# Attention followed by a binarised convolution: the order of the 5x5 products, and where the partial sums are joined

## The chip, the cores and the metric

The kernel runs on one core of one Trainium2 chip. The metric is the device time of one execution in microseconds (us), as the median of three runs. A profile is one further execution, recorded instruction by instruction. Its engines are called PE (TensorE, matmuls; PEld is its weight load), DVE (VectorE), ACT (ScalarE), POOL (GpSimd) and SP (SyncE, which here only issues DMAs).

## What is computed

The input x is 8 images of 64 channels and 64 x 64 pixels, fp32. Two layers follow one another:

```python
# layer 0: attention over the n = 4096 pixels of an image
q, k, v = wq @ xf + bq, wk @ xf + bk, wv @ xf + bv
q_mean, k_mean = q.mean(pixels), k.mean(pixels)
sim = softmax((q - q_mean).T @ (k - k_mean) / 8)
out = sim @ v + v @ softmax(q_mean @ (k - k_mean))   # second term: one vector per image
x = x + out
# layer 1: three binarised convolutions, summed, gated by channel
s = 0
for kk in (1, 3, 5):
    y = sign(x + move_kk)
    z = conv_kk(y, scale * sign(w_kk - mean(w_kk)), padding="SAME")
    s += z * inv_kk + shift_kk                          # batch norm
gate = sigmoid(grouped_linear(mean(s, pixels)))         # channels shuffled
out = s * gate + x
```

## The kernel before

Two images make a pair: their 2 x 64 channels fill the 128 partitions, so there are four pairs. A pair's 4096 pixels are cut into 8 blocks of 512 columns (8 image rows). The outer loop in `attend` runs over the 32 blocks g of all pairs, numbered from 0; the inner one over 32 slots j, one for each 128 keys.

In slot j PE computes `scores` (L472) into a bank pair `ps` of the pool `ps_s`, which has two such buffers, and then `weighted` (L491) for the slot before, which accumulates into `acc`, the only buffer of `ps_a`. ScalarE turns ps into the tile `e` by an exp (L483). VectorE adds each e into `es` (L506), for the softmax's denominators. Matmuls are 64 x 64, so four of them, one for each quarter of the array, run at a time; PE takes them from one queue in program order. In the text, a "stream" is the matmuls that use one half of the array's rows.

Everything else is hung into the slots by `plan`, an explicit table of which function is called after the matmuls of which slot. `put(i, f)` puts f into slot i. The order in which the functions issue their instructions is the order on each engine.

Slot 0 of block g holds `weighted_out` for block g - 1 (ScalarE copies acc to SBUF, L513), the DMAs for the denominators, and then `mix_rows`. This issues one run of matmuls that mixes the queries of block g + 1 (`pq`) with the convolution of block g - 3. Such a convolution is done for blocks g = 3 to 31, so 29 times. Row sums and differences of the signs halve the work: a pair of image rows is put together from four products, named A, B, S and D. The even row of a pair is A + S/2 + D/2 and the odd row -B + S/2 - D/2 (factors `frac`, L206). Each product has 256 columns, two rows' worth of four row pairs.

The PSUM tiles of a convolution are these. z_5 lies in a score buffer of `ps_s` and holds the 5x5's S, A and B. z_5d holds its D and lies in a bank of the pool `ps_m` (two banks). z_3 is the 3x3's A, B, S, D in the buffer of `ps_a`, that is, in the place of acc. z_1, the 1x1 convolution, is in the other bank of `ps_m`. The two banks of `ps_m` are used in turn: first the two query tiles, then the two convolution tiles.

`mix_rows` makes two sequences, `seqs[0]` and `seqs[1]`, for the two streams, and merges them by a running cost: 2.0 for a query, 0.5 for a product, 1.0 for the 1x1. Before the change the first holds 8 products of the 5x5's S, the twelve of the 3x3, the last 2 of S and the 1x1. The second holds 6 of A, the five of D, 4 of A, ten of B.

The sum `sb` of a block is built in this order. When z_5d is complete, `begin_rows` (L719) starts sb with it by two ScalarE operations, one for even and one for odd rows. When z_3 is complete, `hold_rows` (L744) copies it to an SBUF tile, `es_z`, which frees the acc buffer. After the last matmul, `add_rows` (L737) adds S (two operations, even and odd rows), A and B of the 5x5 on VectorE, which frees the score buffer. In slots 7, 8 and 9 `add_held` adds the 3x3's four products from es_z by six more such operations. In slot 10 `end_rows` (L753) adds the 1x1 and accumulates the sum over all pixels into a column of `gap`, for the gate.

The means of a pair come from eight partial sums of its x, made by ScalarE in slots 14 to 28 of an earlier block (L274). `mean_scores`, in slot 0 of blocks 4, 12 and 20, behind `mix_rows`, reduces the eight columns to `xm` on VectorE (L286) and multiplies by a matrix on PE (`pm`, L288). The query tiles are read out right after their matmuls, one by VectorE (`q`, L465) and one by ScalarE (L466). In slot 0 of blocks 1, 8, 16 and 24, behind `mix_rows`, two more small matmuls (`po`, L361 and L362) end a pair's second attention term; VectorE takes the reciprocal of a sum `su` from them and ScalarE checks it (L416).

```python
put(0, both)
if qb == 4 and pr + 1 < n_pairs:
    put(0, lambda: nx().mean_scores(8))
...
    put(7, p3.add_held, b3, "AB")
    put(8, p3.add_held, b3, "S")
    put(9, p3.add_held, b3, "D")
    put(10, p3.end_rows, b3)
```

Of the kernel before, what the change touches and what calls it, by code (L numbers as in the profile page):

```python
# [22 lines left out]
ALU = mybir.AluOpType  # L23
# [21 lines left out]
def conv_seq_kernel(ctx, tc, x, wq, wk, wv, vecs, w1, w3, w5, wtap, gw, out):  # L45
# [211 lines left out]
    class Pair:  # L257
# [3 lines left out]
        def __init__(self, name, xt):  # L261
            self.name, self.x = name, xt
            self.xs = sm.tile([P, 8], F32, tag="xs", name=f"xs_{name}")
            self.q, self.x2, self.s, self.y1, self.acc = {}, {}, {}, {}, {}
            self.es, self.r, self.joint, self.sc = {}, {}, None, None

# [15 lines left out]

        def mean_scores(self, parts=4):

            xm = self.tile(sm, "xm", 0, (P, 1))
            nc.vector.tensor_reduce(xm, self.xs[:, 0:parts], AX.X, ALU.add)  # L286
            self.pm = m_tile(f"pm_{self.name}")
            nc.tensor.matmul(self.pm[:, 0:1], mm, xm, start=True, stop=True)  # L288

# [419 lines left out]
        def sum_tile(self, qb):  # L709
            return bp.tile([P, QB], F32, tag="sb", bufs=9, name=f"sb_{self.name}_{qb}")  # L710

        def begin_rows(self, qb, z):

            self.s[qb] = self.sum_tile(qb)
            if qb == 0:
                self.gap = self.tile(sm, "gap", 0, (P, NQ + 1))
            sv = self.s[qb].rearrange("p (j t w) -> p j t w", t=2, w=HH)
            for t in range(2):
                nc.scalar.activation(  # L719
                    sv[:, :, t, :],  # L720
                    z.rearrange("p (j w) -> p j w", w=HH),
                    AF.Identity,
                    bias=shift,
                    scale=frac[5][:, t : t + 1],
                )

        def add_rows(self, qb, k, name, z):
            sv = self.s[qb].rearrange("p (j t w) -> p j t w", t=2, w=HH)
            f = {
                "A": {0: scale[:, k // 2 : k // 2 + 1]},  # L730
                "B": {1: frac[k][:, 2:3]},
                "S": {0: frac[k][:, 0:1], 1: frac[k][:, 0:1]},
                "D": {0: frac[k][:, 0:1], 1: frac[k][:, 1:2]},
            }[name]
            for t, by in f.items():
                out = sv[:, :, t, :]
                nc.vector.scalar_tensor_tensor(  # L737
                    out, z.rearrange("p (j w) -> p j w", w=HH), by, out, ALU.mult, ALU.add
                )

        def hold_rows(self, qb, two):

            self.z3 = self.tile(sm, "es", f"z3_{qb}", (P, 2, QB))
            nc.scalar.copy(self.z3, two)  # L744

        def add_held(self, qb, names):
            for n in names:
                i = "ABSD".index(n)
                self.add_rows(qb, 3, n, self.z3[:, i // 2, bass.ts(i % 2, QB // 2)])

        def end_rows(self, qb):
            s = self.s[qb]
            nc.vector.scalar_tensor_tensor(  # L753
                s, self.z1, scale[:, 0:1], s, ALU.mult, ALU.add, accum_out=self.gap[:, qb : qb + 1]
            )

        def rows(self, qb):

            return qb * ROWS, ROWS, self.y1[qb], qb

        def joint_rows(self, r0, r1, i):
            y = [t[:, r0 * HH : r1 * HH] for t in self.joint[0]]
            return N // HH - 2 * ROWS + r0, r1 - r0, y, NQ - 2 + i

        def conv_tap(self, rows, z, b, h, n, i, first, last):


            r0, nr, y, _ = rows
# [13 lines left out]

        def convs_out(self, rows, z, n):
            r0, nr, _, col = rows
            w = nr * HH
            qb, at = divmod(r0 * HH, QB)
            if n == 0:
                if qb not in self.s:
                    self.s[qb] = self.sum_tile(qb)
                if qb == 0:  # L790
                    self.gap = self.tile(sm, "gap", 0, (P, NQ + 1))
            s = self.s[qb]
            if self.joint is not None and qb >= NQ - 2:
                s, at = self.joint[1], at + (qb - NQ + 2) * QB
            s = s[:, at : at + w]
            if n == 0:
                nc.scalar.activation(s, z[0][0][:, 0:w], AF.Identity, bias=shift, scale=scale[:, 0:1])
                return
            for h in range(len(z[n])):
                gap = dict(accum_out=self.gap[:, col : col + 1]) if (n, h) == (2, 1) else {}  # L800
                nc.vector.scalar_tensor_tensor(
                    s, z[n][h][:, 0:w], scale[:, n : n + 1], s, ALU.mult, ALU.add, **gap
                )

        def gate_mean(self):
            self.ga = self.tile(sm, "ga", 0, (P, 1))
            some = NQ + (self.joint is not None)
            nc.vector.tensor_reduce(self.ga, self.gap[:, 0:some], AX.X, ALU.add)

# [64 lines left out]
    def mix_rows(q, c):  # L874
# [6 lines left out]
        if c is not None:  # L881
            p, (r0, _, y, qb) = c

            def products(k, name):
                return [((k, name), i, 0.5) for i in range(n_products(k, name))]

            S, A = products(5, "S"), products(5, "A")
            three = [t for name in "ABSD" for t in products(3, name)]
            seqs[0] += S[:8] + three + S[8:] + [((1,), 0, 1.0)]
            seqs[1] += A[:6] + products(5, "D") + A[6:] + products(5, "B")  # L890
        order = []
# [12 lines left out]
        for _, h, b, (n, i, _) in order:  # L904
            if n == ("q",):
                q[0].split_queries(q[1], b, h)
            else:
# [13 lines left out]
                if n == (1,):  # L921
                    p.conv_tap((r0, ROWS, y, qb), [[z[n]]], b, 0, 0, 0, True, True)
                else:
                    p.row_product(z[n], b, *n, i, r0)
            left[n] -= 1
            if left[n] == 0 and n == ("q",):
                q[0].split_queries_out(q[1])
            elif left[n] == 0 and n == (5, "D"):
                p.begin_rows(qb, z[n])
            elif left[n] == 0 and n == (3, "D"):  # L930
                p.hold_rows(qb, z3)
        if c is not None:
            for n in "SAB":
                p.add_rows(qb, 5, n, z[5, n])
            p.z1 = z[1,]

# [20 lines left out]
    def attend(pairs):  # L957
# [9 lines left out]
        def plan(g):  # L967
# [25 lines left out]
            if qb == 4 and pr + 1 < n_pairs:  # L993
                put(0, lambda: nx().mean_scores(8))
                put(0, lambda: nx().mean_scores_out())
                put(1, lambda: nx().value_weights())
# [5 lines left out]
            if g >= 3:  # L1002
                p3, b3 = block(g - 3)
                put(7, p3.add_held, b3, "AB")
                put(8, p3.add_held, b3, "S")
                put(9, p3.add_held, b3, "D")
                put(10, p3.end_rows, b3)
# [43 lines left out]
            if pr + 1 < n_pairs:  # L1051
# [5 lines left out]
                if qb == (3 if pr == 0 else 2):  # L1057
                    for c in range(8):
                        cols = slice(c * QB, (c + 1) * QB)
                        put(14 + 2 * c, lambda c=c, cols=cols: nx().mean_part(c, cols, True))  # L1060
                if qb >= 4:
                    for h in range(2):
# [5 lines left out]
            if g == n_blocks - 1:  # L1068
                put(1, pairs[-1].join)
                put(22, lambda: mix(None, rows(n_blocks - 3), one_bank, score_banks))  # L1070
                put(27, lambda: mix(None, (pairs[-1], pairs[-1].joint_rows(0, 6, 0)), one_bank, score_banks))
            return at
# [33 lines left out]
        for (r0, r1), cols in zip(parts, halves):  # L1106
# [6 lines left out]
            p.signs(b, r0, r1, nc.gpsimd.tensor_copy)  # L1113
        mix(None, (p, p.joint_rows(6, 11, 1)), one_bank, score_banks)
        mix(None, (p, p.joint_rows(11, 16, 2)), one_bank, score_banks)
        p.check(p.r[b], n_blocks - 1)
# [12 lines left out]
    with tc.manual_schedule():  # L1129
# [14 lines left out]
        warm(18)  # L1144
        first.mean_scores(5)
        first.mean_scores_out()
# [16 lines left out]
    with tc.If(n_good < P):  # L1163
        neg = fp.tile([P, QB], F32, tag="e5", name="neg")
        nc.vector.memset(neg, 0.0)
        with tc.For_i(0, n_pairs * P, P) as row:
            rows = bass.ds(row, P)
            p = Pair("g", load_x("g", rows))
            for c in range(4):
                p.mean_part(c, quarters[c])  # L1170
            p.mean_scores()
            p.mean_scores_out()
# [107 lines left out]
```

## Time and profile before

| what | us |
|---|---|
| median of three runs | 1950.62 |
| lowest and highest run | 1950.45, 1952.43 |
| the profiled execution's own time | 1954.38 |
| its span, first to last instruction | 1952.2 |
| PE busy | 1923.2 (99%) |
| DVE busy | 1617.6 (83%) |
| ACT busy | 1275.4 (65%) |
| L506, the additions to es, 960 | 1172.3 |
| L737, `add_rows`, 290 in all | 131.7 |
| L719, `begin_rows`, 58 | 29.6 |
| L744, `hold_rows`, 29 | 29.4 |
| L753, `end_rows`, 29, with its 29 accumulator reads | 24.4 |

A line of the timeline gives the start, the length, the engine, the source line, the operation, what is written and read, the shapes, and how many instructions are merged into the line; in brackets stands how long the engine was idle before it and what it waited for. A fp32 matmul of the kernel is recorded as two instructions, so one slot's scores are eight.

### The profile page before, as it was taken

To read this page: it belongs to the slowest core of one execution; us is meant where nothing else is said; L and a number is where in the kernel's file an instruction comes from. 1 tells how busy PE (TensorE), PEld (TensorE's weight loads), DVE (VectorE), ACT (ScalarE), POOL (GpSimd) and SP (SyncE) were. 2 spreads that over 40 slices of the span, in tenths; PEclk is the share of its full clock that TensorE was granted. 3 is DMA by queue.
4 is the path that set the end of the run, shared out by engine and by line. 5 is a ranking of instruction groups with operands and counts; after the bars stand their busy time and mean duration, and the time that the engine had idled before them with its cause. 6 is when DMAs were issued, how large, how long until landed. Compare 5 with 4: busy or idle time off the path is not lost.

```text
span 1952.2 us, 48415 instructions
## 1 busy us (share of the span) xinstructions
PE 1923.2 (99%) x20848; PEld 800.4 (41%) x20848; DVE 1617.6 (83%) x2066; ACT 1275.4 (65%) x1552; POOL 5.9 (0%) x26
## 2 busy tenths in 40 slices
PE   9999999999999999999999999999999999999997
PEld 4333434443344443444434444344443444444444
DVE  6878878889887888888888888888888888878876
ACT  5667766666666766666666676666666666666663
POOL 0000000000000000000000000000000000000000
PEclk9999999999999999999999999999999999999999
DMA  3021111110102111111011211011111011111111
GB/s 100 31 63 33 29 36 35 38 33 19 40 31 83 56 48 29 36 35 35 28 28 40 80 56 56 16 40 36 35 35 32 23 51 49 55 39 33 28 34 46
DMA packets 58998, 80.58 MB, mean 41 GB/s; under 512 B 15628, under 2 KB 40600, under 8 KB 58648
## 3 DMA queue, kind: packets, MB, share of 16 engines
q1 hardware_dynamic: 58024, 76.22, 12.8%
q8 instruction: 165, 2.70, 0.6%
q10 hardware_dynamic: 720, 1.18, 0.2%
q14 instruction: 57, 0.47, 0.1%
q0 software_dynamic: 32, 0.01, 0.0%
HBM read 39.27 MB, written 24.77 MB: 33 GB/s over the span
## 4 chain that ended last, share of the span: by engine, by line
PE 94%; DVE 3%; ACT 1%; issue 1%; DMA 0%; DVEq 0%; SPq 0%
PE ps L472 44%; PE acc L491 44%; PE z L701 3%; DVE sb L737 2%; PE pv L311 1%; PE pq L458 1%; PE z_5d L701 1%; PE z L775 1%; ACT e L483 0%; DMA x<-in_x 0%; PE warm L155 0%; DVE es L506 0%; DVE r L574 0%; DMA out<-sb 0%; PE pq L430 0%
## 5 line engine op out<-in xcount | busy, mean ns | idle before, releaser
L483 ACT ACTIVATE e<-ps 128x1024 f32<-128x1024 f32 x1024 | 1049.2, 1025 | 621.5 <-PE ps L472 605.9
L506 DVE TENSOR_TENSOR es<-es,e 128x1024 f32<-128x1024 f32 x960 | 1172.3, 1221 | 181.4 <-ACT e L483 151.3
L472 PE MATMUL ps<-q,x 64*64 64x512 f32 x8192 | 1087.0, 592 | 5.4 <-DVE sb L737 4.5
L491 PE MATMUL acc<-e,v 64*64 64x512 f32 x8192 | 1083.9, 590 | 1.2 <-ACT e L483 1.0
L491 PEld LDWEIGHTS acc<-e,v 64*64 64x64 f32 x8192 | 325.6, 131 | 557.6 <-ACT e L483 294.9
L472 PEld LDWEIGHTS ps<-q,x 64*64 64x64 f32 x8192 | 338.9, 133 | 516.1 <-PE ps L472 259.6
L737 DVE SCALAR_TENSOR_TENSOR sb<-z,frac,sb 128x256 f32<-128x256 f32 x87 | 39.2, 478 | 72.5 <-PE z L701 72.5
L701 PE MATMUL z<-ec,wt 64*64 64x256 bf16 x754 | 85.9, 271 | 0.0
L701 PE MATMUL z<-e,wt 64*64 64x256 bf16 x754 | 85.1, 269 | 0.3 <-ACT o L513 0.3
L701 PEld LDWEIGHTS <-wt 64*64 64x64 bf16 x1508 | 77.0, 105 | 1.2 <-issue 0.5
L701 PEld LDWEIGHTS <-wc 64*64 64x64 bf16 x1218 | 62.6, 106 | 6.7 <-issue 0.5
L737 DVE SCALAR_TENSOR_TENSOR sb<-es_z,frac,sb 128x256 f32<-128x256 f32 x145 | 64.8, 481 | 0.0
L701 PE MATMUL z<-ec,wc 64*64 64x256 bf16 x464 | 60.9, 271 | 0.0
L504 DVE TENSOR_TENSOR es<-e,e 128x1024 f32<-128x1024 f32 x32 | 39.2, 1225 | 17.8 <-ACT e L483 17.8
L617 ACT ACTIVATE s<-x,vec 128x512 bf16<-128x512 f32 (+2 forms) x66 | 46.2, 702 | 5.2 <-DVE x L585 5.2
L701 PE MATMUL z<-e,wc 64*64 64x256 bf16 x319 | 44.4, 270 | 0.0
L719 ACT ACTIVATE sb<-z_5d,shift,frac 128x256 f32<-128x256 f32 x58 | 29.6, 561 | 8.9 <-PE z_5d L701 8.9
L513 ACT COPY o<-acc 128x1024 f32<-128x1024 f32 (+2 forms) x33 | 32.3, 981 | 1.2 <-PE acc L491 1.2
L465 DVE TENSOR_SCALAR q<-pq,mx 128x256 f32<-128x256 f32 x30 | 14.5, 484 | 20.7 <-PE pq L458 20.7
L744 ACT COPY es_z<-z 128x1024 f32<-128x1024 f32 x29 | 29.4, 1012 | 0.0
L311 PEld LDWEIGHTS pv<-wx,x 64*64 64x64 f32 x1024 | 22.1, 134 | 17.3 <-issue 8.9
L701 PE MATMUL z<-s,wc 64*64 64x256 bf16 x145 | 26.3, 275 | 0.0
(155 smaller groups left out, 735.8 us busy)
## 6 DMA issues: line engine op xcount, KB each, us to landing
es<-es SPq DMA_DIRECT2D x31, 512.0 KB
e_parts<-es SPq DMA_DIRECT2D x124, 128.0 KB
r<-rc SPq DMA_DIRECT2D x62, 128.0 KB
x<-in_x SPq DMA_DIRECT2D x15, 512.0 KB
out<-sb SPq DMA_DIRECT2D x28, 256.0 KB
ec<-e SPq DMA_DIRECT2D x29, 153.0 KB
xc<-in_x SPq DMA_DIRECT2D x60, 64.0 KB
ec<-e SPq DMA_DIRECT2D x29, 132.0 KB
```

What stands on the lines that cost most here:

```text
L311: nc.tensor.matmul(pv[img[h], b, i * w : (i + 1) * w], self.x[img[b], bass.ds((4 * g + i) * P + h * H, H)], self.wx[img[b], :], start=True ...
L472: nc.tensor.matmul(ps[img[h], b, :], self.x[img[b], bass.ds(j * P + h * H, H)], self.q[qb][img[b], :], start=True, stop=neg is None,)
L483: nc.scalar.activation(e, ps, AF.Exp, scale=1.0 / 8.0)
L491: nc.tensor.matmul(self.acc[qb][img[b], h, :], self.v[img[h], j, img[b]], e[img[h], b, :], start=(j == 0), stop=(j == NK - 1),)
L504: nc.vector.tensor_tensor(self.es[qb], self.first, e, ALU.add)
L506: nc.vector.tensor_tensor(self.es[qb], self.es[qb], e, ALU.add)
L513: nc.scalar.copy(self.acc[qb][:, :, c], acc[:, :, c])
L617: nc.scalar.activation(sy[n][0][:, rows, pad : pad + HH], self.x2[qb][:, r0 * HH : r1 * HH].rearrange("p (h w) -> p h w", w=HH), AF.Sign, ...
L701: nc.tensor.matmul(z[img[b], :].rearrange("p (h w) -> p h w", w=HH), taps[img[h], c * C : c * C + C], src[:, first : first + 3 * step + 1 ...
L719: nc.scalar.activation(sv[:, :, t, :], z.rearrange("p (j w) -> p j w", w=HH), AF.Identity, bias=shift, scale=frac[5][:, t : t + 1],)
L737: nc.vector.scalar_tensor_tensor(out, z.rearrange("p (j w) -> p j w", w=HH), by, out, ALU.mult, ALU.add)
L744: nc.scalar.copy(self.z3, two)
```

## The change

The products are the same. What changes is their order in `mix_rows` and how the sum is put together:

- The first sequence runs the 1x1 right after the first 8 products of S. The second runs all of A, then B, then D.
- `begin_rows` starts sb with the 1x1, by one ScalarE operation.
- `hold_rows` multiplies the 3x3's four products by its half factor while it copies.
- `add_rows` adds the 5x5's A and B to sb and joins its S to the held S, in SBUF: three VectorE operations.
- Slot 7 adds the joined S to even and odd rows. Slot 8 joins the 5x5's D to the held D, reads z_5d for this, and adds it to the even rows and subtracts it from the odd rows. Slot 9 has nothing of this any more. In slot 10 the held A and B are added with factors 2 and -2 and accumulated into two columns of `gap`, which now has 16.
- The reduction to `xm` is a function of its own, `mean_sum`, in slot 30 of the block in which the partial sums are made.

```diff
+        def mean_sum(self, parts=4):
+            self.xm = self.tile(sm, "xm", 0, (P, 1))
+            nc.vector.tensor_reduce(self.xm, self.xs[:, 0:parts], AX.X, ALU.add)
...
         def begin_rows(self, qb, z):
             self.s[qb] = self.sum_tile(qb)
-            for t in range(2):
-                nc.scalar.activation(
-                    sv[:, :, t, :], z.rearrange("p (j w) -> p j w", w=HH),
-                    AF.Identity, bias=shift, scale=frac[5][:, t : t + 1],
-                )
+            nc.scalar.activation(self.s[qb], z, AF.Identity, bias=shift, scale=scale[:, 0:1])
 
+        def hold_rows(self, qb, two):
+            z = self.tile(sm, "es", f"z3_{qb}", (P, 2, QB))
+            nc.scalar.activation(z, two, AF.Identity, scale=frac[3][:, 0:1])
+            self.z3 = [
+                z[:, i // 2, bass.ts(i % 2, QB // 2)].rearrange("p (j w) -> p j w", w=HH)
+                for i in range(4)
+            ]
+
+        def add_rows(self, qb, a, b, s):
+            for out, z, by in zip(self.row_sets(qb), (a, b), (scale[:, 2:3], frac[5][:, 2:3])):
+                z = z.rearrange("p (j w) -> p j w", w=HH)
+                nc.vector.scalar_tensor_tensor(out, z, by, out, ALU.mult, ALU.add)
+            self.join_halves(2, s)
+
+        def join_halves(self, i, z):
+            t = self.z3[i]
+            z = z.rearrange("p (j w) -> p j w", w=HH)
+            nc.vector.scalar_tensor_tensor(t, z, frac[5][:, 0:1], t, ALU.mult, ALU.add)
+
+        def add_halves(self, qb, i):
+            if i == 3:
+                self.join_halves(3, self.z5d)
+            for t, out in enumerate(self.row_sets(qb)):
+                nc.vector.tensor_tensor(
+                    out, out, self.z3[i], ALU.subtract if (i, t) == (3, 1) else ALU.add
+                )
+
+        def end_rows(self, qb):
+            for t, out in enumerate(self.row_sets(qb)):
+                nc.vector.scalar_tensor_tensor(
+                    out, self.z3[t], 2.0 - 4.0 * t, out, ALU.mult, ALU.add, accum_out=self.gap_column()
+                )
...
-            seqs[0] += S[:8] + three + S[8:] + [((1,), 0, 1.0)]
-            seqs[1] += A[:6] + products(5, "D") + A[6:] + products(5, "B")
+            seqs[0] += S[:8] + [((1,), 0, 1.0)] + three + S[8:]
+            seqs[1] += products(5, "A") + products(5, "B") + products(5, "D")
...
-            elif left[n] == 0 and n == (5, "D"):
+            elif left[n] == 0 and n == (1,):
                 p.begin_rows(qb, z[n])
...
-            for n in "SAB":
-                p.add_rows(qb, 5, n, z[5, n])
-            p.z1 = z[1,]
+            p.add_rows(qb, z[5, "A"], z[5, "B"], z[5, "S"])
+            p.z5d = z[5, "D"]
...
-                put(0, lambda: nx().mean_scores(8))
+                put(0, lambda: nx().mean_scores())
...
-                put(7, p3.add_held, b3, "AB")
-                put(8, p3.add_held, b3, "S")
-                put(9, p3.add_held, b3, "D")
+                put(7, p3.add_halves, b3, 2)
+                put(8, p3.add_halves, b3, 3)
                 put(10, p3.end_rows, b3)
...
                         put(14 + 2 * c, lambda c=c, cols=cols: nx().mean_part(c, cols, True))
+                    put(30, lambda: nx().mean_sum(8))
```

More of the change, by code (lines that the diff above doesn't have):

```diff
@@ L264, in __init__ @@
             self.q, self.x2, self.s, self.y1, self.acc = {}, {}, {}, {}, {}
-            self.es, self.r, self.joint, self.sc = {}, {}, None, None
+            self.es, self.r, self.joint, self.sc, self.gap = {}, {}, None, None, None
         def tile(self, pool, tag, i, shape=(P, QB), dtype=F32):
@@ L281, in mean_part, with mean_scores @@
                 nc.vector.tensor_reduce(self.xs[:, c : c + 1], self.x[:, cols], AX.X, ALU.add)
-        def mean_scores(self, parts=4):
-            xm = self.tile(sm, "xm", 0, (P, 1))
-            nc.vector.tensor_reduce(xm, self.xs[:, 0:parts], AX.X, ALU.add)
+        def mean_sum(self, parts=4):
+            self.xm = self.tile(sm, "xm", 0, (P, 1))
+            nc.vector.tensor_reduce(self.xm, self.xs[:, 0:parts], AX.X, ALU.add)
+        def mean_scores(self):
             self.pm = m_tile(f"pm_{self.name}")
-            nc.tensor.matmul(self.pm[:, 0:1], mm, xm, start=True, stop=True)
+            nc.tensor.matmul(self.pm[:, 0:1], mm, self.xm, start=True, stop=True)
         def mean_scores_out(self):
@@ L710, in sum_tile, with gap_column, row_sets @@
             return bp.tile([P, QB], F32, tag="sb", bufs=9, name=f"sb_{self.name}_{qb}")
+        def gap_column(self):
+            if self.gap is None:
+                self.gap, self.n_gaps = self.tile(sm, "gap", 0, (P, 2 * NQ)), 0
+            self.n_gaps += 1
+            return self.gap[:, self.n_gaps - 1 : self.n_gaps]
+        def row_sets(self, qb):
+            sv = self.s[qb].rearrange("p (j t w) -> p j t w", t=2, w=HH)
+            return sv[:, :, 0, :], sv[:, :, 1, :]
         def begin_rows(self, qb, z):
@@ L714, in begin_rows @@
             self.s[qb] = self.sum_tile(qb)
-            if qb == 0:
-                self.gap = self.tile(sm, "gap", 0, (P, NQ + 1))
-            sv = self.s[qb].rearrange("p (j t w) -> p j t w", t=2, w=HH)
-            for t in range(2):
-                nc.scalar.activation(
[L720 to L724, printed above, removed]
-                )
@@ L727, in add_rows @@
[L727 to L736, printed above, removed]
+            nc.scalar.activation(self.s[qb], z, AF.Identity, bias=shift, scale=scale[:, 0:1])
@@ L737, in add_rows @@
+        def end_rows(self, qb):
+            for t, out in enumerate(self.row_sets(qb)):
                 nc.vector.scalar_tensor_tensor(
-                    out, z.rearrange("p (j w) -> p j w", w=HH), by, out, ALU.mult, ALU.add
+                    out, self.z3[t], 2.0 - 4.0 * t, out, ALU.mult, ALU.add, accum_out=self.gap_column()
                 )
-        def hold_rows(self, qb, two):
-            self.z3 = self.tile(sm, "es", f"z3_{qb}", (P, 2, QB))
-            nc.scalar.copy(self.z3, two)
@@ L746, in add_held @@
[L746 to L754, printed above, removed]
-            )
         def rows(self, qb):
-            return qb * ROWS, ROWS, self.y1[qb], qb
-        def joint_rows(self, r0, r1, i):
+            return qb * ROWS, ROWS, self.y1[qb]
@@ L762, in joint_rows @@
+        def joint_rows(self, r0, r1):
             y = [t[:, r0 * HH : r1 * HH] for t in self.joint[0]]
-            return N // HH - 2 * ROWS + r0, r1 - r0, y, NQ - 2 + i
+            return N // HH - 2 * ROWS + r0, r1 - r0, y
         def conv_tap(self, rows, z, b, h, n, i, first, last):
-            r0, nr, y, _ = rows
+            r0, nr, y = rows
             if n == 0:
@@ L783, in convs_out @@
         def convs_out(self, rows, z, n):
-            r0, nr, _, col = rows
+            r0, nr, _ = rows
             w = nr * HH
@@ L789, in convs_out @@
                     self.s[qb] = self.sum_tile(qb)
-                if qb == 0:
-                    self.gap = self.tile(sm, "gap", 0, (P, NQ + 1))
             s = self.s[qb]
@@ L799, in convs_out @@
             for h in range(len(z[n])):
-                gap = dict(accum_out=self.gap[:, col : col + 1]) if (n, h) == (2, 1) else {}
+                gap = dict(accum_out=self.gap_column()) if (n, h) == (2, 1) else {}
                 nc.vector.scalar_tensor_tensor(
@@ L806, in gate_mean @@
             self.ga = self.tile(sm, "ga", 0, (P, 1))
-            some = NQ + (self.joint is not None)
-            nc.vector.tensor_reduce(self.ga, self.gap[:, 0:some], AX.X, ALU.add)
+            nc.vector.tensor_reduce(self.ga, self.gap[:, 0 : self.n_gaps], AX.X, ALU.add)
         def gate(self):
@@ L881, in mix_rows @@
         if c is not None:
-            p, (r0, _, y, qb) = c
+            p, (r0, _, y) = c
+            qb = r0 // ROWS
             def products(k, name):
                 return [((k, name), i, 0.5) for i in range(n_products(k, name))]
-            S, A = products(5, "S"), products(5, "A")
+            S = products(5, "S")
             three = [t for name in "ABSD" for t in products(3, name)]
-            seqs[0] += S[:8] + three + S[8:] + [((1,), 0, 1.0)]
-            seqs[1] += A[:6] + products(5, "D") + A[6:] + products(5, "B")
+            seqs[0] += S[:8] + [((1,), 0, 1.0)] + three + S[8:]
+            seqs[1] += products(5, "A") + products(5, "B") + products(5, "D")
         order = []
@@ L921, in mix_rows @@
                 if n == (1,):
-                    p.conv_tap((r0, ROWS, y, qb), [[z[n]]], b, 0, 0, 0, True, True)
+                    p.conv_tap((r0, ROWS, y), [[z[n]]], b, 0, 0, 0, True, True)
                 else:
@@ L1070, in plan @@
                 put(22, lambda: mix(None, rows(n_blocks - 3), one_bank, score_banks))
-                put(27, lambda: mix(None, (pairs[-1], pairs[-1].joint_rows(0, 6, 0)), one_bank, score_banks))
+                put(27, lambda: mix(None, (pairs[-1], pairs[-1].joint_rows(0, 6)), one_bank, score_banks))
             return at
@@ L1113, in attend @@
             p.signs(b, r0, r1, nc.gpsimd.tensor_copy)
-        mix(None, (p, p.joint_rows(6, 11, 1)), one_bank, score_banks)
-        mix(None, (p, p.joint_rows(11, 16, 2)), one_bank, score_banks)
+        mix(None, (p, p.joint_rows(6, 11)), one_bank, score_banks)
+        mix(None, (p, p.joint_rows(11, 16)), one_bank, score_banks)
         p.check(p.r[b], n_blocks - 1)
@@ L1144, in conv_seq_kernel @@
         warm(18)
-        first.mean_scores(5)
+        first.mean_sum(5)
+        first.mean_scores()
         first.mean_scores_out()
@@ L1170, in conv_seq_kernel @@
                 p.mean_part(c, quarters[c])
+            p.mean_sum()
             p.mean_scores()
```

## The prediction

> **What bounds the kernel now.** I read the page's first two parts, then the chain, then the waits, then the timeline around one convolution. The chain:
>
> ```profile
> span 1952.2 us, 48415 instructions
> PE 1923.2 (99%) x20848; PEld 800.4 (41%) x20848; DVE 1617.6 (83%) x2066; ACT 1275.4 (65%) x1552; POOL 5.9 (0%) x26
> PE 94%; DVE 3%; ACT 1%; issue 1%; DMA 0%; DVEq 0%; SPq 0%
> ```
>
> TensorE sets the time, but 3% of the span, some 60 us, is VectorE work on the chain, 2% at L737 (`add_rows`). The waits say where:
>
> ```profile
> PEld acc L491 <- ACT es_z L744: 11.7, 23, 0.6
> PE pm L288 <- DVE xm L286: 5.9, 3, 2.0
> PE ps L472 <- DVE sb L737: 4.5, 23, 0.2
> ```
>
> (total us, times, longest). These count idle time after the modelled tail of a pipelined matmul, so the real loss is read from starts. Block 5, whose first convolution matmul starts at 313.81, on PE, then ACT and DVE:
>
> ```profile
> 316.51 0.27 PE L701 MATMUL z<-ec,wt 64*64 64x256 bf16 x1
> 316.52 0.63 PE L472 MATMUL ps<-q,x 64*64 64x512 f32 x2
> 316.62 0.27 PE L701 MATMUL z<-ec,wt 64*64 64x256 bf16 x1
> 316.70 1.04 PE L472 MATMUL ps<-q,x 64*64 64x512 f32 x6
> 317.37 1.23 PE L491 MATMUL acc<-e,v 64*64 64x512 f32 x8
> 318.80 1.09 PE L472 MATMUL ps<-q,x 64*64 64x512 f32 x8 [0.20 <-DVE sb L737]
> 319.68 1.07 PE L491 MATMUL acc<-e,v 64*64 64x512 f32 x8
> ...
> 316.30 1.01 ACT L744 COPY es_z<-z 128x1024 f32<-128x1024 f32 x1
> ...
> 316.99 0.88 DVE L737 SCALAR_TENSOR_TENSOR sb<-z,frac,sb 128x256 f32<-128x256 f32 x2 [2.46 <-PE z L701]
> 317.79 0.47 DVE L737 SCALAR_TENSOR_TENSOR sb<-z,scale,sb 128x256 f32<-128x256 f32 x1
> 318.18 0.47 DVE L737 SCALAR_TENSOR_TENSOR sb<-z,frac,sb 128x256 f32<-128x256 f32 x1
> ```
>
> Everywhere else a group of eight starts 0.86 after the one before (319.68 to 320.54 in the next rows). From acc (317.37) to ps (318.80) it is 1.43: **0.57 lost**, because ps needs the score bank that z_5 holds until four L737 operations have read it (last one to 318.66). Acc itself starts 0.06 after the ACT copy ends (317.31), just when PE reaches it: a second limit standing right behind. The same times, to 0.03 us, recur in all 22 ordinary blocks of the 29 with a convolution. Three blocks (4, 12, 20) instead have this:
>
> ```profile
> 731.69 0.27 PE L701 MATMUL z<-ec,wt 64*64 64x256 bf16 x1
> 733.93 0.35 PE L288 MATMUL pm<-xm,mm 128*128 128x1 f32 x2 [1.96 <-DVE xm L286]
> 734.21 1.81 PE L472 MATMUL ps<-q,x 64*64 64x512 f32 x8
> 735.77 1.95 PE L491 MATMUL acc<-e,v 64*64 64x512 f32 x8
> ```
>
> PE stands 2 us while the reduction xm queues behind the four additions, and in blocks 4 and 12 the next two groups then run at half pace (1.56 and 1.71 between starts instead of 0.86).
>
> [...] 99% busy, yet 0.57 lost in most blocks. [...] a 128x512 copy takes 0.586 (L1124), Identity with bias and scale pointers 0.777 (L797). [...] L540 measures 420.
>
> **The change part by part.** PE gets the same matmuls in another order. Let m be the first convolution matmul; one product per stream takes 0.11.
>
> 1. *z_1 takes z_5d's place as the first user of the misc banks.* Before, stream 1 reached z_5d after 6 products and waited 0.13 (314.47 to 314.58) for VectorE's q (ends 314.53). Now z_1 is met after 8 products of stream 0, m+0.88 = 314.69: no wait. z_5d, waiting for ScalarE's q (ends 315.07), comes at m+2.2: none. Stream 1: 25 x 0.11, last start 316.46 instead of 316.62. Stream 0: 8 products, z_1 (512 columns, 0.22), 12 of 3x3, 2 of S: scores follow at m+2.64 = 316.45 and 316.57 (were 316.52, 316.70).
> 2. *begin_rows*: two activations of 0.56 become one of 0.78 (L797's form), at about 315.2 to 316.0, before the held copy: hidden.
> 3. *hold_rows starts later.* z_3 now begins after z_1, at 314.91 (was 314.74); last z_3 316.15; the copy 0.30 later as before: 316.45. It becomes an activation with a scale pointer. Its length is unknown between 1.02 (exp, no pointer) and 1.10 (copy 1.01 plus 0.09); I take 1.10: end 317.55, **acc at 317.61** where PE is ready at 317.31 to 317.43. A new wait of 0.2 to 0.3; behind acc are the next scores and everything on PE.
> 4. *Three operations instead of four release the score bank.* z_5's last product is now S's, 316.37; the additions start 0.37 later, as before: 316.74. A and B at 0.40 apiece to 317.53; joining S to the held tile waits for the copy (317.61) and is read out by 318.09; plus 0.14 as before: bank free 318.23. PE wants it at 317.61+0.86 = **318.47**. The VectorE wait is gone with 0.24 to spare. If A had to wait for D's products as well (0.12 later) nothing changes.
>    Gain: 318.80-318.47 = **0.33 a block**; with 1.02 for the copy 0.41; without the new wait 0.57.
> 5. *Slots 7 to 10.* Before: six L737 (0.40 each back to back) and 0.75+0.09. Now: four tensor_tensor (0.34 to 0.42), a join (0.48), two accumulating operations (0.48+0.09). About 3.1 both ways; costed at nothing. Cover: an exp needs the e tile of five tiles before to be added, and in block 5 the addition for exp 13 (338.83) was done at 333.2, so VectorE may fall 5 us behind before PE hears of it. z_5d's bank is now held to slot 8, z_1's was to slot 10; the next user is slot 13 or the next block. gap grows to 16 columns: a 0.16 reduction, nanoseconds.
> 6. *xm moves to slot 30 of the block before.* ScalarE's last partial sum is issued at slot 28; VectorE has idle gaps there. pm then waits only for begin_rows, long done. No DMA is moved: SP's order is unchanged. pm itself remains: start 0.20 after the last product (as L361's do in block 8), 0.28 to the scores, acc 0.90 after that, ps(2) at m+4.92; block 20 has it at m+7.10. Gain **2.18** x 3 = 6.5. Half-pace recovery: block 4 and 12 are 63.5 from m to m, block 20 is 61.8: 1.7 x 2 = **3.4** in this execution.
>
> Blocks 8, 16, 24 (two po matmuls) lose not at ps but at the next acc, 0.41 late, since ScalarE's check of su waits behind the additions; it comes half a microsecond sooner: 0.5 each. Block 31: z_3 waits for ScalarE's o either way; 0.4.
>
> **Sum.** 22 x 0.33 = 7.3, 3 x 0.5 = 1.5, 0.4, 6.5, 3.4: 19.1. From the profiled execution's own 1954.38 (span 1952.2 and 2.2 around it): 1935.3. That execution is 3.8 above the median, about two half-pace recoveries; the timed runs 1950.45, 1950.62, 1952.43 look like none, none and one of 1.7 (an estimate). For the median I therefore take 15.7: 1950.62-15.7 = **1935**.
>
> **Rivals.**
> *The held copy becomes the limit more strongly.* If z_3 ends later still (0.1 to 0.3 from z_1's wider matmul or waits on its data), each 0.1 is 22 x 0.1 = 2.2 us; with no gain left in ordinary blocks 1943. For: L744 already released acc in 23 blocks. Against: the streams' planned costs balance.
> *The copy does not bind* (PE's starts drift, or 1.02): up to 0.57 a block, 22 x 0.24 = 5.3 more: 1930.
> *Slower: z_1 in mid-stream breaks the four-way pairing.* One stream runs 512 columns while the other runs 256; if each such meeting or the longer A-B run on one stream stalls the other, the cost is per block, and from 15.7/29 = 0.54 us a block the change loses. At 0.8: 1958. For: after a stall the pairs at 314.58 needed three steps to realign. Against: before, z_1 (316.30) ran beside three 256-column products at 0.11 pace with no loss.
> *No effect*: only if additions and xm still wait; the built order shows xm ahead and z_5d's matmuls behind z_5's.
>
> **How the numbers follow.** Forecast as worked out (1931 to 1938) 0.6; copy binding harder (1938 to 1943) 0.2; not binding (1928 to 1931) 0.1; slower 0.07; about nothing 0.03. Range 1929 to 1942; faster 0.9. About 0.2%, 3.9 us, is what a measurement can tell from no change.
>
> **What would show it.** Right: no PE wait on L286; ps(2) released by PE order, not by the additions; acc's weights waiting on es_z for longer; first ordinary-block ps-to-ps distance shorter by 0.3; no half-pace groups. Wrong: conv stretch longer than 2.7 from first to last start, PE ps still waiting on VectorE, exps waiting on VectorE in slots 8 to 14.

## The result and the profile after

The changed kernel takes 1933.88 us, the median of four runs (1933.04 to 1934.54), against 1951.40 for the kernel before (four runs beside them, 1950.45 to 1952.43). The ratio is 0.991, with a 95% interval of 0.9893 to 0.9927. The forecast was 1935, with a range of 1929 to 1942.

The first lines of the page of the profiled execution, and its chain by engine:

```profile
span 1931.8 us, 48355 instructions
PE 1914.2 (99%) x20848; PEld 754.9 (39%) x20848; DVE 1594.1 (83%) x2066; ACT 1274.0 (66%) x1523; POOL 5.9 (0%) x26
PE 97%; DVE 1%; ACT 1%; DMA 0%; issue 0%; SPq 0%; DVEq 0%
```

The span fell by 20.4 us. PE's busy time fell by only 9.0 and its share did not move; the chain shows the gain better. VectorE's part of it went from 3% to 1%, and PE's rose from 94% to 97%. The wait that is left at this place (total us, times, longest):

```profile
PEld acc L493 <- ACT es_z L734: 22.2, 29, 0.9
```

PE's two waits on VectorE, for the score bank (L737 before) and for xm (L286 before), are gone from the list. The wait of acc's weights for the held copy has grown from 11.7 us in 23 blocks to 22.2 in all 29. Block 5 again, in the timeline, PE first, then ACT and DVE. Its first convolution matmul, m, starts at 307.45 (in the kernel before at 313.81); behind the last products stand the first scores, `ps`, then `acc`, then the next `ps`:

```profile
310.12 0.60 PE L474 MATMUL ps<-q,x 64*64 64x512 f32 x2
310.13 0.27 PE L703 MATMUL z_5d<-ec,wc 64*64 64x256 bf16 x1
310.14 0.27 PE L703 MATMUL z_5d<-e,wc 64*64 64x256 bf16 x1
310.24 1.03 PE L474 MATMUL ps<-q,x 64*64 64x512 f32 x6
311.27 1.09 PE L493 MATMUL acc<-e,v 64*64 64x512 f32 x8
312.18 1.04 PE L474 MATMUL ps<-q,x 64*64 64x512 f32 x8
...
308.76 0.78 ACT L729 ACTIVATE sb<-z,shift,scale 128x512 f32<-128x512 f32 x1
310.10 1.11 ACT L734 ACTIVATE es_z<-z,frac 128x1024 f32<-128x1024 f32 x1 [0.56 <-PE z L703]
...
310.40 0.48 DVE L744 SCALAR_TENSOR_TENSOR sb<-z,scale,sb 128x256 f32<-128x256 f32 x1 [2.22 <-PE z L703]
310.80 0.47 DVE L744 SCALAR_TENSOR_TENSOR sb<-z,frac,sb 128x256 f32<-128x256 f32 x1
311.25 0.48 DVE L750 SCALAR_TENSOR_TENSOR es_z<-z,frac,es_z 128x256 f32<-128x256 f32 x1
```

From acc (311.27) to ps (312.18) it is 0.91; before it was 1.43. What is new stands one step earlier: from the first scores at 310.12 to acc it is 1.15, before 0.85, and acc starts 0.06 after the copy ends at 311.21. So the old stall is gone, and a shorter one has come ahead of it, at ScalarE's copy. Block 12, one of the three with pm:

```profile
722.80 0.27 PE L703 MATMUL z_5d<-e,wc 64*64 64x256 bf16 x1
723.00 0.38 PE L290 MATMUL pm<-xm,mm 128*128 128x1 f32 x2
723.32 1.09 PE L474 MATMUL ps<-q,x 64*64 64x512 f32 x8
724.22 1.04 PE L493 MATMUL acc<-e,v 64*64 64x512 f32 x8
```

pm follows the last product by 0.20 where it stood off by 2.24, and no group runs at half pace.

How the 20.4 us of the two profiles are made up, taken from the starts of the first convolution matmul in all 29 blocks:

| where | blocks | before | after | gain |
|---|---|---|---|---|
| ordinary block, m to m (shown: block 5; others are shorter) | 22 | 59.71 | 59.41 | 0.30 each, 6.7 in all |
| with po (block 8) | 3 | 59.42 | 58.85 | 0.57 each, 1.7 |
| with pm (block 20, no half pace) | 3 | 61.78 | 59.65 | 2.13 each, 6.4 |
| half pace after pm (blocks 4 and 12) | 2 | 63.5 | | 1.7 each, 3.4 |
| block 31 to the end | 1 | 92.4 | 92.4 | 0.0 |
| start to block 3's m | | 191.65 | 189.42 | 2.2 |

The last row is not the change's. The first scores matmul of the execution before starts 2.2 later after the first instruction (15.3 against 13.1), in a stretch where both kernels do the same work. The first query matmuls, which wait for the DMA of x, start 0.6 later (7.13 against 6.54); the other 1.6 is the clock, which the trace records as half (0.50) from 7.41 to 10.82 in the kernel before and as full (1.00) all through the first 20 us of the changed one. The changed kernel with the 1x1 one product earlier, below, started as late, at a mean granted clock of 0.997 against 0.998, and had its block 3 at 192.1.

Nor is the row of block 31 quite as empty as it looks. The last instruction that computes ends at m+86.02 before and at m+85.59 after, so 0.43 is gained up to there. Behind it only the last stores are under way, and the time to the end of the span differs from one execution to the next: 6.4 and 6.8 in these two, 6.6 and 6.5 in the first two experiments.

### The profile page after: what moved, and what is told of

Same layout as the page of the kernel before. It is cut to its first block, busy times and chain, and to the rows that moved or that the text cites. A ratio compares the mean times of both kernels' runs of the same rounds, so it can differ in the third digit from the quotient of the medians.

```text
span 1931.8 us, 48355 instructions
## 1 busy us (share of the span) xinstructions
PE 1914.2 (99%) x20848; PEld 754.9 (39%) x20848; DVE 1594.1 (83%) x2066; ACT 1274.0 (66%) x1523; POOL 5.9 (0%) x26
## 4 chain that ended last, share of the span: by engine, by line
PE 97%; DVE 1%; ACT 1%; DMA 0%; issue 0%; SPq 0%; DVEq 0%
PE ps L474 46%; PE acc L493 45%; PE z L703 4%; PE pv L313 1%; PE pq L460 1%; PE z L785 1%; ACT e L485 0%; DMA x<-in_x 0%; DVE es L508 0%; PE warm L155 0%; DVE r L576 0%; PE z_5d L703 0%; DMA out<-sb 0%; ACT o L515 0%; ACT rc_ck L418 0%
## 5 line engine op out<-in xcount | busy, mean ns | idle before, releaser
L474 PE MATMUL ps<-q,x 64*64 64x512 f32 x8192 | 1069.5, 590 | 0.9 <-DVE kb L165 0.9
L493 PE MATMUL acc<-e,v 64*64 64x512 f32 x8192 | 1065.2, 590 | 0.6 <-ACT e L485 0.3
L493 PEld LDWEIGHTS acc<-e,v 64*64 64x64 f32 x8192 | 307.6, 131 | 577.8 <-ACT e L485 305.9
L474 PEld LDWEIGHTS ps<-q,x 64*64 64x64 f32 x8192 | 312.2, 133 | 528.9 <-issue 278.0
L703 PE MATMUL z<-e,wt 64*64 64x256 bf16 x754 | 69.3, 270 | 0.1
L703 PE MATMUL z<-ec,wt 64*64 64x256 bf16 x754 | 69.4, 270 | 0.0
L744 DVE SCALAR_TENSOR_TENSOR sb<-z,scale,sb 128x256 f32<-128x256 f32 x29 | 14.0, 483 | 65.4 <-PE z L703 62.2
L757 DVE TENSOR_TENSOR sb<-sb,es_z 128x256 f32<-128x256 f32 x116 | 43.9, 420 | 1.0
L734 ACT ACTIVATE es_z<-z,frac 128x1024 f32<-128x1024 f32 x29 | 32.3, 1114 | 16.3 <-PE z L703 16.3
L587 DVE SCALAR_TENSOR_TENSOR x<-x,ou,x 128x512 f32<-128x512 f32 (+2 forms) x33 | 24.3, 735 | 1.2
```

The source lines that it names most:

```text
L474: nc.tensor.matmul(ps[img[h], b, :], self.x[img[b], bass.ds(j * P + h * H, H)], self.q[qb][img[b], :], start=True, stop=neg is None,)
L493: nc.tensor.matmul(self.acc[qb][img[b], h, :], self.v[img[h], j, img[b]], e[img[h], b, :], start=(j == 0), stop=(j == NK - 1),)
L587: nc.vector.scalar_tensor_tensor(x2, x2, self.ou, self.x[:, bass.ts(qb, QB)][:, cols], ALU.add, ALU.add)
L703: nc.tensor.matmul(z[img[b], :].rearrange("p (h w) -> p h w", w=HH), taps[img[h], c * C : c * C + C], src[:, first : first + 3 * step + 1 ...
L734: nc.scalar.activation(z, two, AF.Identity, scale=frac[3][:, 0:1])
L757: nc.vector.tensor_tensor(out, out, self.z3[i], ALU.subtract if (i, t) == (3, 1) else ALU.add)
```

## The experiments

All were run beside the kernel before, and each profiled. Times are medians of four or five runs. Between sets of runs the kernel before lay between 1950.67 and 1952.13. The changed kernel was not run again beside them, so differences of a few us from its 1933.88 are read from the traces, where blocks of one kind repeat to some 0.02. "m" is always a block's first convolution matmul; ps(1) and ps(2) are the first and second group of scores behind the convolution.

**xm's reduction alone.** The kernel before with `mean_sum` in slot 30, nothing else:

```diff
-                put(0, lambda: nx().mean_scores(8))
+                put(0, lambda: nx().mean_scores())
...
+                    put(30, lambda: nx().mean_sum(8))
```

> The kernel before with one part of the change alone: the reduction to xm in slot 30 of the block of the partial sums. My theory: blocks 4, 12 and 20 lose their 2 us stall, the additions then end (m+4.85) just when PE asks for the score bank, ps(2) comes at about m+5.1 instead of m+7.1, 2.0 us a block, 6 us in all, and no group runs at half pace any more (up to 1.7 more where a timed run had one): 1943.5 to 1945.5. Ordinary blocks stay at 1.43 from acc to ps. Rival, that the additions take over the stall: at most 1.5 us gained, 1949.5 to 1950.5.

1943.39 (ratio 0.9957, 0.9943 to 0.9970). Blocks 4, 12 and 20 all last 59.78. Block 12:

```profile
726.41 0.38 PE L290 MATMUL pm<-xm,mm 128*128 128x1 f32 x2
726.72 1.09 PE L474 MATMUL ps<-q,x 64*64 64x512 f32 x8
727.63 1.04 PE L493 MATMUL acc<-e,v 64*64 64x512 f32 x8
728.49 1.04 PE L474 MATMUL ps<-q,x 64*64 64x512 f32 x8
```

ps follows acc by 0.86, so the additions do not take over the stall: the score bank comes free just in time behind pm. 3 x 2.0 is 6.0; 7.3 was measured, and the rest is less than one half-pace recovery (1.7) a run; what the clock shows of these stands below. Ordinary blocks are those of before.

**xm's reduction put back.** The changed kernel with `mean_sum(8)` in slot 0, ahead of `mean_scores`:

```diff
-                    put(30, lambda: nx().mean_sum(8))
...
+                put(0, lambda: nx().mean_sum(8))
                 put(0, lambda: nx().mean_scores())
```

> The changed kernel with xm's reduction back in slot 0, behind the additions. My theory: the additions end at m+4.28 instead of m+4.85, so the stall comes back shorter: ps(1) at about m+4.76, ps(2) at m+6.5 against m+4.97, 1.55 us in each of three blocks, 4.7 in all, plus 1.7 for each half-pace recovery (0 to 2): 1938.5 to 1942. Rival, parts that do not overlap (the full 2.1 a block returns): 6.4 without any half pace, 1940.3. Ordinary blocks as in the changed kernel.

1938.34 (0.9933, 0.9920 to 0.9947), 4.5 above the changed kernel. Block 12, and the wait in the list:

```profile
726.03 0.35 PE L290 MATMUL pm<-xm,mm 128*128 128x1 f32 x2 [1.53 <-DVE xm L285]
726.31 1.09 PE L474 MATMUL ps<-q,x 64*64 64x512 f32 x8
...
PE pm L290 <- DVE xm L285: 4.6, 3, 1.5
```

The stall is back, 1.5 long instead of 2.0, because the additions ahead of xm end earlier; the three blocks last 61.22, 1.57 more each, 4.7 in sum. In a block with pm xm's reduction alone gains 2.00 and all the rest alone 0.56, together 2.13: the two parts of the change overlap by 0.43. Nothing ran at half pace after the three stalls of 1.5: in block 12 acc follows ps by 0.91.

**The held copy made shorter.** The 3x3's half factor is left out of this kernel's sums:

```diff
-            nc.scalar.activation(z, two, AF.Identity, scale=frac[3][:, 0:1])
+            nc.scalar.copy(z, two)
```

> The changed kernel with the held copy as a plain copy; the 3x3's half factor is left out of it, so the sums lack it. My theory, that this copy's end releases acc: it is 0.10 shorter (1.01 for 1.11), acc and ps(2) come 0.10 earlier in 22 ordinary blocks and block 31: 2.3 us less, 1931.5. Rival, that PE or VectorE binds there: no change, 1933.9.

**The held copy made longer.**

```diff
-            nc.scalar.activation(z, two, AF.Identity, scale=frac[3][:, 0:1])
+            for i in range(2):
+                nc.scalar.activation(z[:, i, :], two[:, i, :], AF.Identity, scale=frac[3][:, 0:1])
```

> The changed kernel with the held copy in two operations of 512 columns, both after the last 3x3 product, so that only its length changes, by about 0.4 (0.78 twice against 1.11). My theory: acc and ps(2) come 0.4 later in 23 blocks, up to 0.1 later in the three with pm, not later in the three with po: 9 us more, 1943. Rival, that PE's own order sets ps(2) and the copy merely ends near it: under 3 us more, below 1937.

1931.24 for the plain copy (0.9897, 0.9881 to 0.9912) and 1937.80 for the two halves (0.9930, 0.9916 to 0.9943), that is 2.6 less and 3.9 more than the changed kernel. The two copies, the shorter first, each followed by its acc and the next ps:

```profile
309.90 1.01 ACT L734 COPY es_z<-z 128x1024 f32<-128x1024 f32 x1 [0.56 <-PE z L703]
...
310.96 1.09 PE L493 MATMUL acc<-e,v 64*64 64x512 f32 x8
311.87 1.04 PE L474 MATMUL ps<-q,x 64*64 64x512 f32 x8
```

```profile
310.14 1.26 ACT L735 ACTIVATE es_z<-z,frac 128x512 f32<-128x512 f32 x2 [0.56 <-PE z L703]
...
311.46 1.09 PE L493 MATMUL acc<-e,v 64*64 64x512 f32 x8
312.37 1.04 PE L474 MATMUL ps<-q,x 64*64 64x512 f32 x8
```

From the copy's start to acc: 1.06 and 1.32, 1.17 in the changed kernel; from acc to ps: 0.91 in all three. The longer copy was not 0.4 but 0.15 longer, so the expectation of 9 us was wrong in the edit's size and not in its effect: 23 blocks x 0.15 and the three with po, also 0.15 later, which was not expected, give 3.9. Each 0.1 of copy is worth about 2.5 us, in both directions. In ordinary blocks the copy's end sets the pace.

**S added, not joined.** Four operations before the score bank's release, as before:

```diff
-            self.join_halves(2, s)
+            for out in self.row_sets(qb):
+                z = s.rearrange("p (j w) -> p j w", w=HH)
+                nc.vector.scalar_tensor_tensor(out, z, frac[5][:, 0:1], out, ALU.mult, ALU.add)
```

> The changed kernel with the 5x5's S added to even and odd rows of sb by two operations, as before, not joined to the held S: four operations ahead of the score bank's release in place of three. My theory: the held copy, not the additions, sets ps(2). The additions end at about m+4.62 instead of m+4.28 and ps(2) moves from m+4.72 to m+4.77 only: 1 us in 22 ordinary blocks, and 1 us in the three with po, where ScalarE's check waits for them: 1935 to 1936.5. Rival, that the saved operation is the gain: 0.34 to 0.40 in each of 25 blocks, 1942.5 to 1944.

1936.54 (0.9924, 0.9911 to 0.9938), 2.7 more than the changed kernel. Block 5's additions and ps:

```profile
311.62 0.87 DVE L747 SCALAR_TENSOR_TENSOR sb<-z,frac,sb 128x256 f32<-128x256 f32 x2
...
311.69 1.09 PE L493 MATMUL acc<-e,v 64*64 64x512 f32 x8
312.63 1.09 PE L474 MATMUL ps<-q,x 64*64 64x512 f32 x8
```

The additions end at 312.49, 0.33 later than in the changed kernel when both are counted from m, and ps waits for them, but only 0.03 (0.94 after acc for 0.91). Ordinary blocks but one last 0.05 to 0.12 longer, those with po 0.33, where ScalarE's check stands behind the additions. So of the operation that was saved, nearly all is hidden in an ordinary block: four operations from the earlier start, m+2.95, end at m+4.61, against m+4.85 in the kernel before, and that brings the release of the bank to within 0.03 of the copy's limit. No room is left, though: in block 25 VectorE starts the additions 0.35 late, ps comes as much later, and the block lasts 0.41 longer than in the changed kernel.

**D between A and B.**

```diff
-            seqs[1] += products(5, "A") + products(5, "B") + products(5, "D")
+            seqs[1] += products(5, "A") + products(5, "D") + products(5, "B")
```

> The changed kernel with D between A and B in the second stream, so that z_5 is complete only with the last matmul. Theory 1, from the order: D now comes at m+1.1, before ScalarE has read out its half of the queries (m+1.26), and the wait of 0.2 in PE's one queue holds up the 3x3 products and the held copy behind it: ps(2) 0.1 to 0.2 later in 25 blocks, 1936.5 to 1939. Theory 2, that D's place matters only through the start of the additions, which are not the limit: 1934 to 1934.5.

1937.82 (0.9927, 0.9913 to 0.9940), 3.9 more. z_5d, which has taken the bank that ScalarE reads the queries from, comes too early:

```profile
308.87 0.27 PE L703 MATMUL z<-ec,wt 64*64 64x256 bf16 x1
309.07 0.27 PE L703 MATMUL z_5d<-e,wc 64*64 64x256 bf16 x1
309.07 0.29 PE L703 MATMUL z_5d<-ec,wc 64*64 64x256 bf16 x1
309.08 0.30 PE L703 MATMUL z<-e,wt 64*64 64x256 bf16 x1
```

Both streams pause until 309.07, 0.20 after the product before, where one product follows another by 0.11 elsewhere. The convolution's last start moves from m+2.69 to m+2.90, the held copy from m+2.65 to m+2.78, and ps by the same 0.13. The order is worth its 0.13 a block through PE's queue; the additions start 0.33 later, at m+3.28, end at m+4.55 and still do not decide. Taken with the run before: the earlier start alone brings the additions to within 0.03 of the copy's limit, and the saved operation alone puts them inside it, so neither is the gain by itself.

**The 1x1 one product earlier.**

```diff
-            seqs[0] += S[:8] + [((1,), 0, 1.0)] + three + S[8:]
+            seqs[0] += S[:7] + [((1,), 0, 1.0)] + three + S[7:]
```

> The changed kernel with the 1x1 after 7 of S's products, 3 left for the end: the 3x3 and the held copy come one product, 0.11, earlier. z_1's bank is free at m+0.78, and the 1x1 comes at m+0.77, so it should not wait. My theory: acc and ps(2) 0.10 earlier in 23 blocks, 1931.5. Rival, that z_1 then waits for VectorE and the gain is lost: 1933.5 to 1934.5.

1933.12 (1931.77 to 1934.51; 0.9901, 0.9886 to 0.9916). The trace agrees with the first theory: the copy starts at m+2.56, ps comes at m+4.63 for m+4.72, ordinary blocks last 59.31 for 59.41, some 2 us in all. The median is only 0.8 lower, between theory and rival, but the four runs are two near 1931.8 and two near 1934.4. The profiled execution is one of the latter, 1934.51, and has the late start, 2.7 after the changed kernel's (15.76 against 13.06). So the 2 us of the blocks stand in the trace, and the median hides them.

**The held copy in two halves, two tiles.** acc's two banks become two tiles of `ps_a`, so that each is released by itself, and the first half of the copy is issued after the 3x3's B:

```diff
-            nc.scalar.activation(z, two, AF.Identity, scale=frac[3][:, 0:1])
+            nc.scalar.activation(z[:, i, :], two[i], AF.Identity, scale=frac[3][:, 0:1])
...
-                nc.scalar.copy(self.acc[qb][:, :, c], acc[:, :, c])
+                for h in range(2):
+                    nc.scalar.copy(self.acc[qb][:, h, c], acc[h][:, c])
...
-                        z3 = ps_a.tile([P, 2, QB], F32, tag="acc", name=f"z{name}")
+                        z3 = acc_banks(f"z{name}")
...
-            elif left[n] == 0 and n == (3, "D"):
-                p.hold_rows(qb, z3)
+            elif left[n] == 0 and n in ((3, "B"), (3, "D")):
+                p.hold_rows(qb, z3, "BD".index(n[1]))
...
+    def acc_banks(name):
+        return [ps_a.tile([P, QB], F32, tag=f"acc{h}", name=f"{name}_{h}") for h in range(2)]
```

> The changed kernel with acc's two banks as two tiles and the held copy in two halves, the first (3x3's A and B) issued as soon as B is complete, so that only the second half lies behind the last product. The copy of acc to o is in halves as well (0.2 more of ScalarE, and some 0.4 at the end). My theory: the second half ends at about m+3.53 instead of m+3.76, acc at m+3.6, PE's own pace and the additions (m+4.28+0.14) then set ps(2) at m+4.45 to 4.5: 0.22 to 0.27 in 23 blocks, 1928 to 1929.5. Rival, that the extra ScalarE work comes back as later exps: no gain or a loss, 1934 or more.

1929.94 (0.9886, 0.9871 to 0.9901): 3.9 less than the changed kernel, and 0.4 above the range of the theory. Its block 5, where m is 307.87:

```profile
309.85 1.35 ACT L737 ACTIVATE es_z<-z,frac 128x512 f32<-128x512 f32 x2
...
311.38 1.15 PE L493 MATMUL acc<-e,v 64*64 64x512 f32 x8
312.24 1.15 PE L474 MATMUL ps<-q,x 64*64 64x512 f32 x8
...
PEld acc L493 <- ACT es_z L737: 3.9, 22, 0.3
```

The second half ends at 311.20, m+3.33, earlier than expected; acc comes at m+3.52 and ps 0.86 later: PE's own pace. The wait on es_z shrinks from 22.2 to 3.9. ps comes 0.34 earlier after m. Of the 22 ordinary blocks eight gain as much in their period, 0.31 to 0.35; nine, block 5 among them, gain 0.24 (59.17 for 59.41) and five 0.11 to 0.23. Those with po gain 0.01 and those with pm lose 0.12. From block to block the trace gains 5.3 in sum, its span 4.0: it starts 0.6 later than the changed kernel's, with the first scores at 13.70, and from block 31's m to the end it takes 0.6 longer, all of it behind the last instruction that computes.

**Both of the last two.** Their diffs together.

> The last two edits together: held copy in halves, and the 1x1 after 7 of S's products. With the halves alone ps(2) stands 0.86 after acc, which is PE's own pace, and acc no longer waits. My theory: nothing is left for the earlier copy to release, so ordinary blocks keep ps(2) at m+4.38 and the time is that of the halves alone, 1929 to 1931. Rival, that the copy still sets the pace: another 2 us, 1927.5 to 1928.

1929.40 (1928.74 to 1931.24; 0.9889, 0.9872 to 0.9905). The copy ends 0.1 earlier still and ps stays at m+4.38. There is nothing left for it to release.

## Why the prediction was right

Step by step, counted from m:

| step | forecast | measured |
|---|---|---|
| 1: first scores | 2.64 | 2.66 |
| 2: begin_rows | 1.4 to 2.2 | 1.31 to 2.09 |
| 3: held copy, start and length | 2.64, 1.10 | 2.65, 1.11 |
| 3: acc | 3.80 | 3.81 |
| 4: additions end | 4.28 | 4.28 |
| 4: ps(2), ordinary block | 4.66 | 4.72 |
| 6: ps(2), block with pm | 4.92 | 4.97 |
| po block, gain | 0.5 | 0.57 |

The mechanism was right in each step, the two that went against the change included: the copy that starts later and the pointer operand that lengthens it. The pointer's price can be estimated from the kernel before: Identity with two pointers (0.777, L797) is 0.191 longer than a copy of the same shape (0.586, L1124), about 0.10 for each if the two cost alike; the forecast took 0.09. The held copy with one pointer took 1.114, without it 1.01, so 0.10. Step 5's 0.42 for a tensor_tensor of 256 columns is that of L540 in the kernel before; the new ones (L757) took 0.42 as well.

The first term that was mis-sized is acc to ps in step 4. I took 0.86, as in the stretches without a wait. Behind a wait it is 0.91, in the changed kernel and in both kernels with another copy. That costs 0.05 in 22 blocks, 1.1 us. Some of it comes back at once: in the kernel before, the acc behind the old wait stood 0.88 after ps (318.80 to 319.68), not 0.86, and that 0.02 is gone too. So a block gains 0.30 of the forecast 0.33. Why groups behind a wait follow a little later was not tested. One sign came out smaller than forecast: from ps(1) to ps(2) it is 2.06 for 2.28, 0.22 shorter and not 0.3. Block 31 gained its 0.4, up to the last computing instruction, and the scatter of the stores hid it.

The second mis-sized term is the half pace. For the median I had left recoveries out, since the three runs of before looked like none, none and one. 17.5 us were gained where 15.7 were forecast, and the block terms without half pace sum to only 14.8 (6.7, 1.7 and 6.4 of the table). That leaves 2.7, and the records of the clock hold most of it.

Up to its last 10 us the trace of the kernel before has a half clock in three stretches of 3.41 us, from 7.41, 256.58 and 734.45, each at 0.50 and so worth 1.7; the prediction saw the last two and not the one in the start. Without the three the profiled execution would have taken 1949.3, an estimate, and the lowest of all runs of this kernel took 1950.31: none of them looks free of it. The timed runs have no trace, but their mean granted clock is on record, and a stretch lowers it by 0.0009 (half of 3.41 in 1952, an estimate). For 25 runs of the kernel before, taken beside the experiments, it averages 0.9961; for the changed kernel and the eight experiments other than the 1x1 one product earlier, 41 runs, 0.9971. The difference is worth 1.9 us a run, an estimate; the other 0.8 stays open, and so does which of these stretches lay in the start, which the change does not touch.

That the forecast came as near as 1.1 us is in part luck: it had the blocks' gain too large by 0.9, put the lost clock at nothing, and started from a median of three runs 0.8 lower than that of four.

Of the rivals, the copy as a stronger limit did not happen: z_3 ended where the order says. That it does not bind was refuted by the shorter and the longer copy. Mid-stream z_1 did no harm: from first to last start the convolution takes 2.69, and took 2.81. VectorE's slots 7 to 10 were costed at nothing. Exps waited for VectorE's es additions nine times and for 6.2 us in all, against three times and 2.1; before, four more had waited for `add_held` (2.6). Seven of the nine stand at slot 14, which the prediction had named as a sign of being wrong. But the blocks in which they stand gain as much as the others (block 9 0.29, block 17 0.29), so none of it is seen to reach PE.

## What to carry to other kernels

When a stall goes, look at what was ready just behind it: here acc came 0.06 after a copy's end, with no loss before, and the copy became the next limit as soon as its input came later. Count stalls from start to start and not from idle time: the list of waits showed 4.5 us where block periods could give back some 12.5 (22 blocks x 0.57, by the prediction's measure of acc to ps, 1.43 for 0.86); with the copy in halves the 22 blocks did give back 12.3. And a reader that releases a buffer in one piece can be halved, if each half has its own tile; then the first half's copy lies under the second half's matmuls: here acc's wait for the copy fell from 22.2 us to 3.9.

## What was not expected

Two ScalarE operations of 128x512 from PSUM with a scale pointer, one behind the other, take 1.26 together, only 0.15 more than one of 128x1024 (1.11). I had taken 0.78 for each, the row of `begin_rows`, which has a bias pointer besides; with the scale pointer alone one takes 0.68, and two overlap by 0.10 (2 x 0.68 less 1.26).

The half pace does not follow from the length of a stall alone. Each of the three stretches of half clock in the kernel before begins soon after PE has gone on from a stall of nearly 2 us, and lasts 3.41. A fourth stall of that length has none behind it:

| where | PE waits for | stall | PE goes on | granted clock behind |
|---|---|---|---|---|
| before, start | DMA of x | 1.96 | 7.13 | 0.50 from 7.41 to 10.82 |
| before, block 4 | xm | 1.98 | 255.38 | 0.50 from 256.58 to 259.99 |
| before, block 12 | xm | 1.96 | 733.93 | 0.50 from 734.45 to 737.86 |
| before, block 20 | xm | 1.97 | 1212.46 | 1.00 |
| changed kernel, start | DMA of x | 1.39 | 6.54 | 1.00 |
| xm put back, block 12 (4 and 20 alike) | xm | 1.53 | 726.03 | full pace: 0.91 from ps to acc |

So the half clock came 0.28, 1.20 and 0.52 after PE went on. This is why in block 4 the first scores behind pm still run at full pace (0.91 to the next group) and the two groups behind them do not (1.69 and 1.71). Why block 20's stall went without it, and what length of stall is short enough, is not shown.
